# A graph and convolution layer on one core: tap weights transformed channel by channel, and eight neighbour parts moved beside the first frequency products

## The chip, the cores and the metric

The kernel runs on one NeuronCore of a Trainium2 chip, in float32. The metric is device time in microseconds. The run before the change takes 2466.53 us (median of three, 2464.61 to 2470.27). One more execution was recorded by the hardware profiler; the profile and the trace are of that one.

The engines are TensorE (PE; its weight loads are shown apart as PEld), VectorE (DVE), ScalarE (ACT), GpSimd (POOL) and SyncE (SP). Each works through its own queue in the order in which the program issued. SyncE, GpSimd and ScalarE also issue DMAs.

## The reference, cut to what matters

`x` is [128 graphs, 128 nodes, 256 channels], `adj` [128, 128, 128]. The layer that the change touches is the first:

```python
h = relu(layernorm(x))                       # the layer's input, per graph
c = relu(bn1(conv1d(h, conv1_w, pad=0)))     # one tap: a 256x256 product
c = bn2(conv1d(c, conv2_w, pad=8))           # 17 taps along the 128 nodes, 256 -> 256 channels
x_conv = relu(c + h)
s = h @ w_se.T + b_se                        # 3 numbers per node
A = exp(-|s_n - s_m|^2) * adj                # neighbour weights
x_nmp = A @ relu(h @ w_msg.T + b_msg)
x = x + gru([x_conv, x_nmp], h)              # gates r, z, n from w_ih (768x512) and w_hh (768x256)
```

A second layer then works on the first 25 nodes of each graph: five small normalised graph convolutions, summed.

## The kernel before, in words

The 128 graphs are 32 groups q of four (`GB`), in four batches of eight groups (`BQ`). The 17-tap convolution is done in frequency space. A graph's 128 nodes are cut into four overlapping blocks of 48 points (`F`), which a fixed matrix `fwd` transforms; a matrix `inv` transforms back. For each of the 24 frequency pairs the 256x256 product over channels has a real and an imaginary part.

The parts are generators. Each yields a pair: the TensorE time of what it has just issued, and a delay before its next step. `Order.run` (lines 187 to 205) merges two lanes of such generators with these numbers: it picks the lane that is behind by its weight, and in it the generator that is ready first. This sets the order of all instructions when the program is built. Nothing of it is decided on the chip.

- `stage_a(q)`, lines 326 to 372: load x as xa (L318), layernorm on DVE with one small power on POOL, eight transposes ph (L340) and relu to hTa (L342), a store to hTd (L345), the first convolution pc (L351), its bias on DVE (L354) and relu on POOL (L356), then the forward transform pf (L362), copied to X by DVE and ACT (L368, L370).
- `load_taps` and `tap_weights`, lines 375 to 406: four loads of conv2_w, with the 17 taps as partitions, a group of 32 partitions for each quarter of the input channels. Thirty-two steps of four products pw (L394) follow: the constant `tap` [17, 72] is the stationary operand, two input channels with all 256 outputs the moving one. Output partitions are the 72 slots: two for the first pair of frequencies, and three for each of the other 23 (a real part, minus the sum, and a difference). ACT and DVE copy to ws (L401, L399), which has two buffers, and POOL stores it to wfd in DRAM (L403).
- `stage_b(bat)`, lines 409 to 463: for each pair of frequencies load the weights wf from wfd (L418, two DMAs, 1 KB pieces), let POOL form the sum xs of real and imaginary input (L425), and multiply: pa = xs by the first weight (L450), pb = the two parts by the other two (L453). y is the copy pac of pa, added to both halves of pb (L457), and is stored to yd (L459).
- `stage_c(q)`, lines 485 to 635: its first part is the neighbour part: pse (L498), its scaled copies ef (L503, L506), their product lr on POOL (L509), messages pm and msg (L518 to L522), distances pd (L532), transposed adj pt (L534), aT (L536, L537), and x_nmp as px and xnmp (L546, L548). Then it loads yt from yd and transforms back (pi, L562), computes the gates (L581 to L608), transposes back (po, L620), adds x and stores.
- `setup_1`, `prepare`, `block`, from line 640: the second layer, in eight blocks of 16 graphs.

At the start, batch 0's `stage_a` runs beside `tap_weights` (line 875). Then `groups`, which is `stage_c` of all 32 groups, runs beside `side`, which is `stage_b(0)`, then batch 1's `stage_a` and `stage_b`, and so on, at weight 0.5 (line 888); then groups beside the second layer at weight 0.4 (line 889). `stage_c(q)` may begin once group q-1 has its last gates, so beside `stage_b(0)` there is group 0's neighbour part and no other.

Of the kernel before, what the change touches and what calls it, by code (L numbers as in the profile page):

```python
# [9 lines left out]
FP = mybir.dt.float32  # L10
# [9 lines left out]
P = 128  # L20
# [10 lines left out]
NSLOT = 72  # L31
# [29 lines left out]
def _fourier():  # L61
# [8 lines left out]
    tap = np.zeros((TAPS, NSLOT))  # L70
# [17 lines left out]
    for f in range(1, NF + 1):  # L88
        th = 2 * np.pi * ((f * t) % F) / F
        vr, vi = np.cos(th), np.sin(th)  # L90
        tap[:, 3 * f - 1], tap[:, 3 * f], tap[:, 3 * f + 1] = vr, -(vr + vi), vi - vr
    tap4 = np.zeros((P, NSLOT))
# [116 lines left out]
def kernel(ctx: ExitStack, tc: tile.TileContext, x, adj, consts, vecs, w_se, conv1_w,  # L209
# [11 lines left out]

    hTd = [dr.tile([P, 2, 512], FP, name=f"hTd{q}") for q in range(NQ)]
    wfd = dr.tile([NSLOT, D, D], FP, name="wfd")
# [31 lines left out]

    scl, sft = {}, {}
    for bn in ("bn1", "bn2"):
        s = cp.tile([P, 2], FP, name=f"s_{bn}")
        nc.vector.tensor_scalar(s, v(bn + "_v"), EPS, None, op0=ALU.add)
        nc.gpsimd.tensor_tensor(s, s, c("mhalf")[:, :2], ALU.pow)  # L260
        nc.vector.tensor_mul(s, s, v(bn + "_g"))
        t = cp.tile([P, 2], FP, name=f"t_{bn}")
        nc.vector.tensor_mul(t, v(bn + "_m"), s)
        nc.vector.tensor_sub(t, v(bn + "_b"), t)
        scl[bn], sft[bn] = s, t
    brz = cp.tile([P, 4], FP, name="brz")
    nc.vector.tensor_add(brz, v("b_ih")[:, 0:4], v("b_hh")[:, 0:4])


    prow = ptmp.tile([P, 4, P], FP, tag="tmp", name="prow")  # L270
    for i, a in enumerate((scl["bn1"][:, 0:1], scl["bn1"][:, 1:2], sft["bn1"][:, 0:1],
                           sft["bn1"][:, 1:2])):
        wide = f2.tile([P, P], FP, tag="wide", name=f"wide{i}")
        nc.vector.tensor_copy(wide, a.to_broadcast([P, P]))
        nc.tensor.matmul(prow[:, i], wide, ident, start=True, stop=True)
    brow = cp.tile([P, D], FP, name="brow")
    nc.vector.tensor_copy(brow, prow[:, 2:4].rearrange("p a c -> p (a c)"))
    for k in range(2):
        nc.vector.tensor_mul(c1w[:, k], c1w[:, k], prow[:, 0:2].rearrange("p a c -> p (a c)"))


    wse9 = wp.tile([P, 2, WIDE], FP, name="wse9")
    nc.vector.memset(wse9, 0.0)
    for role in range(3):
        nc.vector.tensor_copy(wse9[:, :, 3 * role:3 * role + 3], wse[:, :, :3])
    pbs = ptmp.tile([P, 512], FP, tag="tmp", name="pbs")
    nc.tensor.matmul(pbs[:, :1], c("sel"), v("b_se"), start=True, stop=True)
    bse = cp.tile([P, 1], FP, name="bse")
    nc.vector.tensor_copy(bse, pbs[:, :1])
    emb = c("emb")  # L290
    embb = cp.tile([P, 4], FP, name="embb")
    nc.vector.scalar_tensor_tensor(embb, emb[:, 4:8], bse, emb[:, 8:12],
                                   op0=ALU.mult, op1=ALU.add)
# [14 lines left out]


    lab = ExitStack()  # L310
    ab = lab.enter_context(tc.tile_pool(name="ab", bufs=2, side="right"))
    xf = lab.enter_context(tc.tile_pool(name="xf", bufs=1, side="right"))
    X = xf.tile([P, 2, F, P], FP, name="X")
# [12 lines left out]
    def stage_a(q):  # L326
# [8 lines left out]
        yield 0.0, 8.0  # L335
# [8 lines left out]
        yield 0.9, 2.5  # L344
        nc.gpsimd.dma_start(out=hTd[q], in_=hT)  # L345
        h1 = ab.tile([P, GB, D], FP, tag="h1", name=f"h1{q}")
        for h in range(2):
# [8 lines left out]
            nc.gpsimd.tensor_scalar(h1[:, s], h1[:, s], 0.0, None, op0=ALU.max)  # L356
            yield 1.75, 2.5 * h
# [17 lines left out]
    def load_taps(tw):  # L375

        wts = []
        for n in range(4):
            wt = tw.tile([P, 16, D], FP, tag="wt", name=f"wt{n}", bufs=4)
            src = conv2_w.rearrange("(r n i) t o -> n t r i o", r=4, n=4)[n]  # L380
            for r in range(4):
                nc.sync.dma_start(out=wt[32 * r:32 * r + 16], in_=src[:16, r])
            nc.sync.dma_start(out=wt[16::32], in_=src[16])
            wts.append(wt)
        return wts

    def tap_weights(tw, wts):
        for n in range(4):
            for m in range(8):
                st = tw.tile([NSLOT, 4, 512], FP, tag="ws", name=f"ws{n}_{m}")  # L390
                for r in range(4):
                    pw = pacc.tile([P, 512], FP, tag="acc", name=f"pw{n}_{m}_{r}")
                    rows = slice(32 * r, 32 * r + TAPS)
                    nc.tensor.matmul(  # L394
                        pw[:NSLOT], c("tap")[rows],
                        wts[n][rows, 2 * m:2 * m + 2].rearrange("t i o -> t (i o)"),
                        start=True, stop=True)
                    if r == 3:
                        nc.vector.tensor_copy(st[:, r], pw[:NSLOT])  # L399
                    else:  # L400
                        nc.scalar.activation(st[:, r], pw[:NSLOT], AF.Copy)  # L401
                i0 = 16 * n + 2 * m
                nc.gpsimd.dma_start(  # L403
                    out=wfd.rearrange("s (r i) o -> s r i o", r=4)[:, :, i0:i0 + 2],
                    in_=st.rearrange("s r (i o) -> s r i o", i=2))
                yield 0.9, 1.2


    def stage_b(bat):
        while not all(q in A_DONE for q in range(bat * BQ, (bat + 1) * BQ)):  # L410
            yield 0.0, 0.5
        WF = {}

        def load_w(f):
            w = WF[f] = xf.tile([P, 2, 3, D], FP, tag="wf", name=f"wf{bat}_{f}", bufs=3)
            a, n = (0, 2) if f == 0 else (3 * f - 1, 3)
            for k in range(2):
                nc.sync.dma_start(out=w[:, k, :n],  # L418
                                  in_=wfd[a:a + n, k * P:(k + 1) * P].rearrange("s p o -> p s o"))
# [511 lines left out]
```

## Time and profile before

| what | us |
|---|---|
| median of three runs | 2466.53 |
| the profiled execution, whole | 2468.99 |
| its span, first to last instruction | 2467.2 |
| TensorE busy | 2299.7 (93%) |
| GpSimd, VectorE, ScalarE busy | 790.4, 751.2, 606.6 |
| mean granted clock of TensorE | 0.961 |
| tap products pw, first and last start | 24.7, 177.4 |
| first product of stage b(0) | 212.1 |
| first back transform pi | 300.1 |

A float32 product is two entries for TensorE in this profile, each with its own weight load, so 736 entries of pb are 368 products. A busy TensorE is not always at full speed: PEclk gives the share of the full clock that it was granted. A line such as `PE pd L532 <- POOL lr L509: 17.7, 6, 9.2` says that TensorE waited six times before pd for POOL's lr, 17.7 us in all, the longest 9.2. A line of the chain gives the start, the length, and what ran or was waited for.

### The profile page before, as it was taken

What the parts mean: (1) busy time and instruction counts of PE and PEld (TensorE: products, weight loads), DVE (VectorE), ACT (ScalarE), POOL (GpSimd) and SP (SyncE); (2) the same over time, 40 slices, a digit from 0 to 9 for tenths busy, and PEclk for the clock granted to TensorE, in tenths of its full rate; (3) what the DMA queues carried; (4) which work ended last, traced back from release to release, by engine and by line L of the source; (5) the groups of instructions that cost most, each with busy time, mean ns of one, the idle gap of its engine ahead of it and who ended that gap; (6) DMA issues with size and microseconds to landing.
All of it is one profiled execution on the core that took longest, in us unless ns stands there. A gap on an engine that the chain in (4) does not pass through costs nothing.

```text
span 2467.2 us, 26809 instructions
## 1 busy us (share of the span) xinstructions
PE 2299.7 (93%) x10156; PEld 1509.3 (61%) x10156; DVE 751.2 (30%) x1603; ACT 606.6 (25%) x1149; POOL 790.4 (32%) x976
## 2 busy tenths in 40 slices
PE   3878799998998999999998999999999999999998
PEld 2447655566665666666666666656566665656576
DVE  2333311333223244222343222232232232322343
ACT  1441122222221212222222222222223222232223
POOL 1333323343333234333334333332222232323231
PEclk9779899999999999999999999999999999999999
DMA  9657911233545322555423355611211212120000
GB/s 166 189 164 257 301 43 60 74 89 94 170 159 174 82 52 86 162 179 175 119 77 99 117 171 177 184 44 43 60 38 38 73 31 68 48 55 20 20 21 18
DMA packets 207538, 258.86 MB, mean 105 GB/s; under 512 B 21805, under 2 KB 179378, under 8 KB 207410
## 3 DMA queue, kind: packets, MB, share of 16 engines
q1 hardware_dynamic: 175154, 172.07, 25.8%
q0 software_dynamic: 30208, 81.30, 10.7%
q10 hardware_dynamic: 2048, 3.79, 0.5%
q8 instruction: 80, 1.31, 0.2%
q14 instruction: 48, 0.39, 0.1%
HBM read 175.82 MB, written 81.26 MB: 104 GB/s over the span
## 4 chain that ended last, share of the span: by engine, by line
PE 79%; DMA 3%; DVE 3%; POOL 3%; issue 3%; ACT 2%; SPq 0%; DVEq 0%; POOLq 0%; ACTq 0%
PE pr L581 13%; PE pz L581 13%; PE pn L581 9%; PE pb L453 6%; PE pg L581 4%; PE pi L562 4%; PE pz L812 4%; PE ph L803 4%; PE pc L351 3%; PE pa L450 3%; PE pm L518 3%; PE pf L362 3%; PE px L546 2%; DMA wf<-wfd 1%; PE ph L340 1%
## 5 line engine op out<-in xcount | busy, mean ns | idle before, releaser
L604 POOL TENSOR_TENSOR d<-hT,r 128x512 f32<-128x512 f32 x64 | 80.8, 1263 | 547.6 <-ACT r L596 339.3
L453 PE MATMUL pb<-wf,X 128*128 128x256 f32 x736 | 173.9, 379 | 0.0
L457 DVE TENSOR_TENSOR y<-pac,pb 128x512 f32<-128x512 f32 x92 | 63.2, 687 | 334.1 <-PE pb L453 330.5
L605 POOL TENSOR_TENSOR d<-d,z 128x512 f32<-128x512 f32 x64 | 81.1, 1267 | 257.2 <-ACT z L601 221.1
L453 PEld LDWEIGHTS pb<-wf,X 128*128 128x128 f32 x736 | 139.9, 190 | 19.0
L562 PE MATMUL pi<-cst,yt 96*128 96x64 f32 x1024 | 125.5, 283 | 21.1 <-DMA yt<-yd 21.1
L562 PEld LDWEIGHTS pi<-cst,yt 96*128 96x128 f32 x1024 | 124.2, 201 | 22.8 <-issue 22.6
L596 ACT ACTIVATE r<-r,vec 128x512 f32<-128x512 f32 x64 | 46.2, 722 | 355.5 <-DVE r L595 355.5
L581 PE MATMUL pr<-hT,whh 128*128 128x512 f32 x256 | 129.1, 629 | 0.0
L356 POOL TENSOR_SCALAR h<-h 128x512 f32<-128x512 f32 x64 | 95.5, 1501 | 90.8 <-DVE h L354 90.1
L518 PE MATMUL pm<-wmsg,hT 128*128 128x256 f32 x512 | 122.6, 389 | 2.1 <-ACT ef L506 2.1
L351 PE MATMUL pc<-c1w,hTa 128*128 128x256 f32 x512 | 124.1, 395 | 0.0
L581 PE MATMUL pr<-xnmp,wih 128*128 128x512 f32 x256 | 121.7, 598 | 2.4 <-DVE xnmp L548 2.4
L581 PE MATMUL pr<-xc,wih 128*128 128x512 f32 x256 | 121.1, 595 | 0.0
L581 PE MATMUL pz<-hT,whh 128*128 128x512 f32 x256 | 121.0, 595 | 0.0
L581 PE MATMUL pg<-hT,whh 128*128 128x512 f32 x256 | 120.6, 593 | 0.0
L581 PE MATMUL pn<-xnmp,wih 128*128 128x512 f32 x256 | 120.3, 592 | 0.0
L581 PE MATMUL pz<-xnmp,wih 128*128 128x512 f32 x256 | 120.3, 592 | 0.0
L581 PE MATMUL pz<-xc,wih 128*128 128x512 f32 x256 | 120.3, 592 | 0.0
L581 PE MATMUL pn<-xc,wih 128*128 128x512 f32 x256 | 120.3, 592 | 0.0
L803 PE MATMUL ph<-yz,w 128*128 128x96 f32 (+3 forms) x640 | 113.8, 332 | 4.1 <-ACT aT L536 1.6
L591 DVE SCALAR_TENSOR_TENSOR r<-pg,vec,r 128x512 f32<-128x512 f32 x64 | 48.0, 750 | 228.1 <-PE pg L581 145.8
(156 smaller groups left out, 3771.3 us busy)
## 6 DMA issues: line engine op xcount, KB each, us to landing
wf<-wfd SPq DMA_DIRECT2D x184, 384.0 KB, 4.0
yd<-y POOLq DMA_DIRECT2D x96, 256.0 KB, 4.2
yt<-yd SPq DMA_DIRECT2D x32, 768.0 KB, 7.6
wfd<-ws POOLq DMA_DIRECT2D x32, 576.0 KB, 5.6
xa<-in_x SPq DMA_DIRECT2D x128, 128.0 KB, 4.5
hTd<-hTa POOLq DMA_DIRECT2D x32, 512.0 KB, 3.2
hT<-hTd SPq DMA_DIRECT2D x32, 512.0 KB, 3.4
xt<-in_x SPq DMA_DIRECT2D x128, 128.0 KB, 2.7
```

The lines of the kernel that those rows point to most:

```text
L351: nc.tensor.matmul(pc[:, i], hT[:, k, (2 * h + i) * N:(2 * h + i + 1) * N], c1w[:, k], start=(k == 0), stop=(k == 1))
L356: nc.gpsimd.tensor_scalar(h1[:, s], h1[:, s], 0.0, None, op0=ALU.max)
L362: nc.tensor.matmul(pf[:, i, :F * NB], h1[:, 2 * h + i, k * P:(k + 1) * P], fwd, start=True, stop=True)
L450: nc.tensor.matmul(pa, xs[:, k], w[:, k, 0], start=(k == 0), stop=(k == 1))
L453: nc.tensor.matmul(pb[:, s], X[:, k, 2 * f + part], w[:, k, 1 + s], start=(k == 0), stop=(k == 1))
L518: nc.tensor.matmul(pm[:, i], hT[:, k, j * N:(j + 1) * N], wmsg[:, k], start=(k == 0), stop=(k == 1))
L562: nc.tensor.matmul(pc[:, a * 64:(a + 1) * 64], yt[:, a, co * P:(co + 1) * P], inv[:HB], start=True, stop=True)
L581: nc.tensor.matmul(ps, w, a, start=(i == 0), stop=(i == len(ops) - 1))
L604: nc.gpsimd.tensor_sub(d, hT[:, dc], r)
L605: nc.gpsimd.tensor_mul(d, d, z)
L803: nc.tensor.matmul(ph, w1[:, g, k, m * P:(m + 1) * P], yz[:, k, :, o:o + n], start=(k == 0), stop=(k == 1))
L812: nc.tensor.matmul(pz, w2[:, g, m, cc * P:(cc + 1) * P], hs[g][:, m], start=(m == 0), stop=(m == 3))
```

## The change

Six things change.

1. The tap transform. The input channels become the output partitions. The stationary operand is now the taps of 128 input channels for one output channel (17x128, at a step of 64 floats), the moving one the constant `tap`, now [17, 48]. It is done in two halves k of the input channels, for four quarters r of the output channels, 64 channels each, in seven chunks of 10 or 9 channels. A chunk has four accumulators, and each is copied into ws[r] with its two free axes exchanged. ws[r] has one buffer; a half ends with four stores of [128, 48x64].
2. Two weights are stored for each frequency pair, real and imaginary. Stage b loads both with one DMA (512-byte pieces) and POOL forms the third as their sum. pa now holds the two products of the parts, pb that of the sums, and y is formed by two differences and a sum on DVE.
3. The neighbour part becomes a function of its own, `neighbours`. For groups 0 to 7 a new generator, `early`, runs it beside the end of stage a and beside stage b(0), and stores its result to xmd. `stage_c` loads that in place of adj for these groups. Loads of w_ih and w_hh move from ACT's queue to the end of `tap_weights` on SyncE's.
4. The folding of the batch norms into weights moves from the start of the program into a generator `fold`, the first of the second lane. Stage a's lane has weight 2.
5. The relu after the first convolution goes from POOL to ACT, and lr from POOL to DVE. Some delays in the yields are shorter.
6. In `block`, turn, gather and fuse are issued in a mixed order, the first hidden tile gets a tag of its own (hh0), and zt has three buffers instead of four.

```diff
     for f in range(1, NF + 1):
         th = 2 * np.pi * ((f * t) % F) / F
-        vr, vi = np.cos(th), np.sin(th)
-        tap[:, 3 * f - 1], tap[:, 3 * f], tap[:, 3 * f + 1] = vr, -(vr + vi), vi - vr
+        tap[:, 2 * f], tap[:, 2 * f + 1] = np.cos(th), np.sin(th)
...
+    wfd = dr.tile([P, 8, F, CQ], FP, name="wfd")
+    xmd = [dr.tile([P, 2, 512], FP, name=f"xmd{q}") for q in range(BQ)]
...
-            nc.gpsimd.tensor_scalar(h1[:, s], h1[:, s], 0.0, None, op0=ALU.max)
-            yield 1.75, 2.5 * h
+            nc.scalar.activation(h1[:, s], h1[:, s], AF.Relu)
+            yield 1.75, 1.6 * h
...
+    def tap_weights():
+        mid = ExitStack()
+        tw = mid.enter_context(tc.tile_pool(name="tw", bufs=2))
         wts = []
+        for k in range(2):
+            wt = tw.tile([P, P, CQ], FP, tag="wt", name=f"wt{k}")
+            src = conv2_w[k * P:(k + 1) * P].rearrange("i t (r o) -> r t i o", r=4)
             for r in range(4):
+                nc.sync.dma_start(out=wt[32 * r:32 * r + 16], in_=src[r, :16])
+            nc.sync.dma_start(out=wt[16::32], in_=src[:, 16])
             wts.append(wt)
+        yield 0.0, 4.0
+        bounds = [0, *range(10, CQ + 1, 9)]
+        for k in range(2):
+            ws = [tw.tile([P, F, CQ], FP, tag=f"ws{r}", name=f"ws{k}_{r}", bufs=1)
+                  for r in range(4)]
+            for a, b in zip(bounds, bounds[1:]):
+                pws = [pacc.tile([P, b - a, F], FP, tag="acc", name=f"pw{k}_{a}_{r}")
+                       for r in range(4)]
+                for i in range(a, b):
+                    for r in range(4):
+                        rows = slice(32 * r, 32 * r + TAPS)
+                        nc.tensor.matmul(pws[r][:, i - a], wts[k][rows, :, i], c("tap")[rows],
+                                         start=True, stop=True)
                 for r in range(4):
+                    dst = ws[r][:, :, a:b].rearrange("p s c -> p c s")
+                    if r == 1:
+                        nc.vector.tensor_copy(dst, pws[r])
                     else:
+                        nc.scalar.activation(dst, pws[r], AF.Copy)
+                yield 0.22 * (b - a), 1.5
+            for r in range(4):
+                nc.gpsimd.dma_start(out=wfd[:, 4 * k + r], in_=ws[r])
+        mid.close()
+        wg = ctx.enter_context(tc.tile_pool(name="wg", bufs=1, reuse_waits="tile"))
+        LATE["wih"] = weight(wg, w_ih, [P, 4, 3 * D], "(k p) o -> p k o", "wih", nc.sync)
+        LATE["whh"] = weight(wg, w_hh, [P, 2, 3 * D], "(k p) o -> p k o", "whh", nc.sync)
...
     def stage_b(bat):
...
+        while "xf" not in LATE:
+            yield 0.0, 0.5
+        if bat == 0:
+            yield 0.0, 12.0
...
         def load_w(f):
-            w = WF[f] = xf.tile([P, 2, 3, D], FP, tag="wf", name=f"wf{bat}_{f}", bufs=3)
+            w = WF[f] = xf.tile([P, 8, 3, CQ], FP, tag="wf", name=f"wf{bat}_{f}")
+            nc.sync.dma_start(out=w[:, :, :2], in_=wfd[:, :, 2 * f:2 * f + 2])
...
+        def add(f):
+            XS[f] = xf.tile([P, 2, P], FP, tag="xs", name=f"xs{bat}_{f}", bufs=2)
+            nc.gpsimd.tensor_tensor(XS[f], X[:, :, 2 * f], X[:, :, 2 * f + 1], ALU.add)
+            nc.gpsimd.tensor_tensor(WF[f][:, :, 2], WF[f][:, :, 0], WF[f][:, :, 1], ALU.add)
+
+        def product(ps, xk, f, s):
             for k in range(2):
+                nc.tensor.matmul(ps.rearrange("p (o c) -> p o c", c=CQ), xk(k),
+                                 WF[f][:, 4 * k:4 * k + 4, s], start=(k == 0), stop=(k == 1))
...
+            pa = pacc.tile([P, 2, D], FP, tag="acc", name=f"pa{bat}_{f}")
+            for s in range(2):
+                product(pa[:, s], lambda k: X[:, k, 2 * f + s], f, s)
...
+                nc.scalar.activation(pac, pa, AF.Copy)
+                pb = pacc.tile([P, D], FP, tag="acc", name=f"pb{bat}_{f}")
+                xs = XS.pop(f)
+                product(pb, lambda k: xs[:, k], f, 2)
+                nc.vector.tensor_sub(y[:, 0], pac[:, 0], pac[:, 1])
+                nc.vector.tensor_add(pac[:, 0], pac[:, 0], pac[:, 1])
+                nc.vector.tensor_sub(y[:, 1], pb, pac[:, 0])
...
-        nc.gpsimd.tensor_tensor(lr, ef[:, 0::2], ef[:, 1::2], ALU.mult)
+        nc.vector.tensor_tensor(lr, ef[:, 0::2], ef[:, 1::2], ALU.mult)
...
+    def early(q):
+        while q not in A_DONE:
+            yield 0.0, 0.5
+        if q == 0:
+            load_c(0)
+            yield 0.0, 6.0
+        hT, ad = IN.pop(q)
+        if q + 1 < BQ and q + 1 in A_DONE:
+            load_c(q + 1)
+        xm = LATE["fr"].tile([P, 2, 512], FP, tag="xnmp", name=f"xnmp{q}", bufs=2)
+        yield from neighbours(q, hT, ad, xm)
+        nc.gpsimd.dma_start(out=xmd[q], in_=xm)
...
+        for what, q in ((turn, 0), (turn, 1), (turn, 2), (gather, 0), (gather, 1), (fuse, 0),
+                        (turn, 3), (gather, 2), (fuse, 1), (gather, 3), (fuse, 2), (fuse, 3)):
...
-    with tc.tile_pool(name="tw", bufs=2) as tw:
-        load_xa(0)
-        load_xa(1)
-        taps = load_taps(tw)
-        order.run(Lane([stage_a(q) for q in range(BQ)], ahead=2), Lane([tap_weights(tw, taps)]))
...
-    first, second = [stage_b(0)], [setup_1()]
+    load_xa(0)
+    begin = Lane([stage_a(q) for q in range(BQ)], ahead=2, weight=2.0)
+    beside = Lane([fold(), tap_weights()] + [early(q) for q in range(BQ)])
+    order.run(begin, beside, until=begin)
+    order.run(Lane([stage_b(0)]), beside)
+    first, second = [], [setup_1()]
```

## The prediction

> **What bounds the kernel now.** I read the page's slices first, then busy time by windows, then the chain of waits, then who waits for whom. The slices:
>
> ```profile
> PE   3878799998998999999998999999999999999998
> PEclk9779899999999999999999999999999999999999
> DMA  9657911233545322555423355611211212120000
> ```
>
> A slice is 61.7 us. From the sixth on TensorE is full, so only taking work off it or filling its small gaps helps there. The first five are not full, and their clock is low. The windows:
>
> ```profile
> 20.00:40.00 20.00, 7.74 (x24) 2.33 (x24) 4.92 (x15) 3.12 (x6) 2.61 (x3) 1.00 1.17 108
> 80.00:100.00 20.00, 16.22 (x55) 6.07 (x53) 11.01 (x33) 8.14 (x17) 5.50 (x7) 0.71 0.41 122
> 140.00:160.00 20.00, 16.66 (x54) 6.03 (x52) 10.82 (x33) 7.81 (x16) 5.50 (x7) 0.66 0.42 123
> 240.00:260.00 20.00, 19.24 (x88) 15.97 (x87) 4.81 (x7) 2.93 (x8) 8.52 (x14) 1.00 1.00 338
> 280.00:300.00 20.00, 8.37 (x36) 6.21 (x34) 9.15 (x28) 1.15 (x3) 4.22 (x6) 0.83 0.90 251
> ```
>
> The last three figures are granted clock, DMA share and GB/s. At 20 to 40 us the tap loads fill the DMA at only 108 GB/s; from 60 to 200 us TensorE seems busy, at 0.66 to 0.9 of its clock; at 240 the weight loads of stage b fill the DMA. Who waits:
>
> ```profile
> ACT ws L401 <- DMA wfd<-ws: 74.9, 17, 14.3
> DVE ws L399 <- DMA wfd<-ws: 58.5, 14, 11.9
> PE pw L394 <- ACT ws L401: 34.9, 15, 12.7
> PE pd L532 <- POOL lr L509: 17.7, 6, 9.2
> ```
>
> And the chain:
>
> ```profile
> 158.11 6.11 DMA wfd<-ws
> ...
> 164.33 0.60 ACT ws L401
> ...
> 173.95 5.16 DMA wfd<-ws
> ...
> 232.08 7.29 DMA wf<-wfd
> ...
> 289.73 3.90 DMA yd<-y
> ...
> 293.78 6.16 DMA yt<-yd
> ...
> 300.07 7.06 PE pi L562 x32
> ```
>
> Each of 32 tap steps waits for the staging write of two steps before (133 us of waits on ACT and DVE); stage a's products stand behind it on TensorE. Stage b(0) starts at 212 us, waits for wf four times, and group 0's first inverse product runs at 300.1. By then TensorE did, at full clock: stage a 8 x 7.2 = 57 us (eight transposes 1.0 as in po; eight products 3.65 as in pm; eight of 192 columns 2.6, half of pf's 5.21), taps about 32 x 1.06 = 34, b(0) 62 (a step is 0.86 + 1.73 us in the chain), one neighbour part 7.0 (0.57 + 3.65 + 0.43 + 0.59 + 1.78). That is 160 of 300 us: 140 to win. After it, 2167.1 us hold 2082 us of busy TensorE.
>
> [...] The new tap load has pieces of 256 B (64 floats) instead of 1 KB; no run shows such a load. [...] pd, four row groups, issues its eight loads within 0.31 us, four products in 0.43. [...] The new tap weights are read at a step of 256 B, and evicted at such a step; no row of before does either.
>
> **The change, part by part.** I followed the yields through Lane and Order to get the new order of issue. Times below are on TensorE's clock of events up to group 0's first pi.
>
> *Start.* SyncE now issues xa0, xa1, xa2 before the taps; eight such issues took 8.06 us, so the taps start at about 13 us. One half of the channels is 2.23 MB: 21 us at 107 GB/s. [...] I take 1.3: first tap product at 40 us, between 34 and 56. The tap products stand first in TensorE's queue, ahead of a(1)'s transposes, so nothing hides this. xa3 stands behind both halves on SyncE: it lands near 40 + 27 + 3, and its layernorm (5 us) ends at 75, against a need near 72: 3 us.
>
> *Tap products.* 128 channels-of-four: 512 products of 48 columns with 128 weights, four row groups. pi, of 64 columns, is bound by its loads: 32 of them in 3.65 us later on, two a product, 0.23 us. Below: that pair, perfectly fourfold: 0.23 us a four, 29 us. Above: no overlap, 0.91, 117 us. [...] I take 0.33: 42 us, 8 more than now.
>
> *Evictions.* 56 of 128x432 or 480 instead of 128 of 72x512: about 0.57 on ACT (hh 128x400 is 0.593), 33 us in all instead of 72. All four accumulators belong to one chunk, so two chunks issued one after the other cost about 2.1 us; my order has three such pairs besides the one below, and stage a covers the rest. [...] 14 us, between 6 and 40 (a doubled eviction at the wide step).
>
> *Between the halves.* ws has one buffer for each row group, 1.57 MB each. The first chunk of the second half follows the four writes directly, and its evictions wait for them; behind them on ACT stand hTa's copies of a(4), on TensorE the next chunk and a(4). 32 KB of x1d land in 2.0 us and 512 KB of hTd in 3.2, which is up to 400 GB/s; I take 340, so 6.3 MB and a fixed 2 us are 20.5 us, less the chunk's 3: 18 us idle, between 12 and 28. New, and uncovered.
>
> So stage a and taps end at 40 + 57 + 42 + 14 + 3 + 18 = 174 us, against 212.
>
> *Handover.* The writes of the second half (6.3 MB) run beside wih, whh and the first hT and adj (3.1 MB): 25 us at 370 GB/s, the rate of before at 214 to 290. wf's first load waits for all writes, then 5 us; load_c of group 2 stands behind it on SyncE and is not needed yet. hT comes after some 17 us, so neighbour 0 and half of 1 (9.6 us) fill the gap. First product of b(0) 32 us after the last tap: 206, plus or minus 8.
>
> *b(0) beside neighbours.* 62 + 46 (the other 6.6 parts) = 108 us. Loads fall from 768 to 512 KB a step, but in pieces of 512 B; with yd, hT, adj and xmd 28 MB in 108 us is 260 GB/s, under the 334 of now. POOL's sum of weights (as d, 1.26 us) waits for wf; behind it on POOL stand only the yd issue and the xmd store. I add 8 us for waits (2 to 22): 322. Then yd, yt and group 0: 12 us as now, of which a(9)'s first 2.7 us fill some: pi at 334.
>
> *The rest.* 2167.1 us less seven neighbour parts (49), less a(9)'s 2.7, less half the wait for lr and what relu on POOL (1.5 us against 0.63 on ACT) cost: 10. POOL loses 95.5 + 23.8 us and gains 92 x 1.26 = 116; DVE gains 92 x (3 x 0.41 - 0.69) + 13 = 63 (0.41 from the 128x256 adds); ACT 40 + 20. All lie beside full TensorE (DVE 30%, ACT 25%, POOL 32% busy); if the new sums make TensorE wait, 0 to 15 us, so the gain here is between -5 and 20. Turn, gather and fuse in another order: TensorE's waits there are under 3 us, so nothing. 2105.
>
> Sum: 334 + 2105 = 2439 of span, 1.8 around it (2468.99 - 2467.2): 2441 against 2468.99. The profiled run is 2.5 above the median, so I forecast 2439 against 2466.5, 1.1% faster.
>
> **Rivals.** *Tap loads in small pieces (slower).* Place: wt on SyncE, with xa3 behind. At 2.5 times the time per byte the first half lands at 66, the second at 119, xa3's layernorm is done at 128 against a need at 98: 26 + 27 more than forecast, 2492. It decides from about 1.9 times on; 4 times gives 2556. For: [...] the queue is full at 1.17 already. [...]
> *Tap weights load one after another, or at half rate for the wide step.* At 0.91 us a four, 74 us more, of which waits between the halves and for xa3 absorb 9: 2504. Half rate, fourfold, 0.46 a four, gives 2456. Against: pd's fourfold overlap.
> *The gain is lost to DMA.* Writes at 200 GB/s (12 + 13 us more) and b(0) bound by 512 B pieces (14): 2478 less what neighbours fill, about 2466: no change.
> *More of the old loss goes* ([...] taps 0.23, lr's and relu's waits gone): 2405.
>
> **How the numbers follow.** Forecast 0.55, its own range 2415 to 2460; better 0.06; lost to DMA 0.11; small pieces 0.16; slow weights 0.12. A measurement tells apart some 0.2%, 5 us. Faster: 0.55 less its upper edge, plus 0.06, plus 0.03 from the DMA case: 0.60. Same 0.08, slower 0.32. Range 2400 to 2510: it leaves out part of the better case and the far ends of the slow ones.
>
> **What would show it.** First pw near 40 us (over 50: small pieces); a four of tap products at 0.33; one wait of TensorE of about 18 us in the middle of stage a for ws; first product of b(0) near 206; first pi near 334; no pse, pm or px among groups 0 to 7 later; no wait of pd for POOL. The forecast is wrong if tap loads or tap products hold TensorE, or if after 334 us more than 2125 remain.

## The result, and the profile after

The changed kernel takes 2484.74 us (median of four runs, 2479.94 to 2486.72), the kernel before, in the runs beside it, 2465.57: a ratio of 1.0071, 95% interval 1.0051 to 1.0091. It is 0.7% slower where 1.1% faster was forecast. The profiled execution has a span of 2483.9 us and a mean granted clock of 0.954. One of the five executions of a later version, e15, took 10390 us; its ratio is that of the other four.

The 40 slices of the changed kernel:

```profile
PE   3968989999999889998999999899999999999998
PEclk9768989999999899999999999999999999999999
DMA  9255872335553334444125445212121121212000
```

The second and fifth slices are fuller than before, the third less full, and the clock in the second to fourth is 0.7, 0.6 and 0.8: TensorE is busy there for much of the time, and slow. The same stretches by windows (TensorE, its weight loads, DVE, ACT, POOL; then clock, DMA share, GB/s):

```profile
20.00:40.00 20.00, 2.55 (x10) 2.28 (x10) 6.65 (x31) 0.00 (x0) 1.70 (x2) 1.00 1.26 95
80.00:100.00 20.00, 16.62 (x167) 15.23 (x168) 6.19 (x15) 8.87 (x13) 2.13 (x3) 0.59 0.32 106
140.00:160.00 20.00, 16.97 (x168) 15.48 (x168) 2.88 (x3) 8.51 (x12) 1.06 (x2) 0.59 0.56 194
240.00:260.00 20.00, 20.00 (x122) 17.32 (x121) 12.77 (x21) 5.72 (x13) 13.25 (x16) 1.00 0.83 251
280.00:300.00 20.00, 19.86 (x140) 16.86 (x139) 14.11 (x24) 5.42 (x13) 9.53 (x13) 1.00 0.84 274
```

In the first of them the tap loads, now in 256-byte pieces, run at 95 GB/s where 1 KB pieces ran at 108. In the windows from 80 and from 140 us the mean granted clock is 0.59, with the weight loads (second figure) almost as busy as the products. Stage b(0), from 240, is full (20.00 and 19.86 of 20 us) at a clock of 1.00 in its two windows, as forecast. The waits of TensorE:

```profile
PE pw L404 <- ACT ws L411: 18.1, 6, 8.9
PE px L561 <- DVE aT L553: 18.1, 7, 12.1
PE pw L404 <- DMA wt<-in_conv_w: 17.5, 1, 17.5
...
PE pw L404 <- DVE ws L409: 9.3, 3, 3.5
...
PE pd L548 <- DVE msg L537: 4.0, 2, 2.0
...
PE pd L548 <- DVE lr L525: 3.4, 2, 1.7
```

The waits of pw for ws, on ACT and DVE together, fell from 37.0 us (34.9 and 2.1) to 27.4, of which 18.0 are a new wait between the two halves; pd's wait for lr fell from 17.7 to 3.4. So the waits that the change was to remove did go. The wait of px for aT rose from 7.7 us to 18.1, 12.1 of them in one place, at 1184 us; the same wait of 12.1 us stands in e1, e3, e4, e10, e11 and e16, and no run tries what makes it. From the chain that ended last:

```profile
25.79 15.78 DMA wt<-in_conv_w
...
127.37 14.89 DMA wfd<-ws
...
213.19 5.49 DMA wfd<-ws
...
230.10 4.37 DMA wf<-wfd
...
343.11 6.87 DMA yd<-y
...
351.78 6.37 DMA yd<-y
358.30 5.91 DMA yt<-yd
364.34 5.96 PE pi L610 x32
```

The tap load is in it once, the write of the first half's ws once (at 127), and the end of b(0) is a row of yd, yd, yt. Group 0's first pi comes at 364.3, not at 300.1 as before and not at 334 as forecast; after it 2119.6 us remain, where before it was 2167.1 and 2105 were forecast. Stage by stage against the forecast's own sum:

| step | forecast, us | measured, us | difference |
|---|---|---|---|
| first tap product | 40 | 41.7 | +1.7 |
| from there to the end of stage a and taps | 134 | 170.0 (to 211.7) | +36.0 |
| handover to b(0)'s first product | 32 | 22.8 (to 234.5) | -9.2 |
| b(0) | 116 | 113.2 (to 347.7) | -2.8 |
| to group 0's first pi | 12 | 16.6 (to 364.3) | +4.6 |
| the rest | 2105 | 2119.6 | +14.6 |
| sum (span) | 2439 | 2483.9 | +44.9 |

Two rows make the miss: the tap stage and the rest. Together they are 50.6 us over; that the handover and b(0) were priced 12 us too high hides a part of it.

### The profile page after: what moved, and what is told of

The parts are those of the page before. It is cut to its first block, busy times and chain, and to the rows that moved or that the text cites. A ratio compares the mean times of both kernels' runs of the same rounds, so it can differ in the third digit from the quotient of the medians.

```text
span 2483.9 us, 28406 instructions
## 1 busy us (share of the span) xinstructions
PE 2310.1 (93%) x10924; PEld 1563.8 (63%) x10924; DVE 886.1 (36%) x1801; ACT 634.8 (26%) x1145; POOL 778.2 (31%) x956
## 4 chain that ended last, share of the span: by engine, by line
PE 78%; DVE 6%; issue 5%; DMA 4%; POOL 3%; ACT 3%; SPq 1%; DVEq 0%; POOLq 0%; ACTq 0%
PE pr L630 13%; PE pz L630 12%; PE pn L630 9%; PE pa L449 6%; PE pc L357 5%; PE pi L610 4%; PE pg L630 4%; PE ph L853 4%; PE pz L862 4%; PE pf L368 3%; PE pb L449 3%; PE px L561 2%; PE pm L534 2%; PE pw L404 1%; PE ph L346 1%
## 5 line engine op out<-in xcount | busy, mean ns | idle before, releaser
L653 POOL TENSOR_TENSOR d<-hT,r 128x512 f32<-128x512 f32 x64 | 81.1, 1267 | 507.1 <-ACT r L645 280.2
L449 PE MATMUL pa<-wf,X 128*128 128x256 f32 x768 | 188.2, 389 | 9.4 <-DMA wf<-wfd 9.4
L449 PEld LDWEIGHTS pa<-wf,X 128*128 128x128 f32 x768 | 147.9, 196 | 53.8 <-issue 28.4
L473 DVE TENSOR_TENSOR y<-pac 128x256 f32<-128x256 f32 x92 | 65.0, 707 | 275.8 <-ACT pac L469 273.5
L654 POOL TENSOR_TENSOR d<-d,z 128x512 f32<-128x512 f32 x64 | 81.1, 1268 | 230.0 <-ACT z L650 196.2
L444 POOL TENSOR_TENSOR wf<-wf 128x512 f32<-128x512 f32 x92 | 123.8, 1346 | 46.2 <-DMA wf<-wfd 46.1
L357 PE MATMUL pc<-c1w,hTa 128*128 128x256 f32 x512 | 135.3, 424 | 0.0
L272 POOL TENSOR_TENSOR rs<-rs,cst 128x4 f32<-128x4 f32 x40 | 40.8, 1021 | 294.1 <-DVE rs L271 294.1
L357 PEld LDWEIGHTS pc<-c1w,hTa 128*128 128x128 f32 x512 | 108.9, 216 | 24.9 <-issue 5.8
L650 ACT ACTIVATE z<-pz,brz 128x512 f32<-128x512 f32 x64 | 44.0, 687 | 282.0 <-PE pz L630 282.0
```

Source lines behind the costliest of these rows:

```text
L357: nc.tensor.matmul(pc[:, i], hT[:, k, (2 * h + i) * N:(2 * h + i + 1) * N], c1w[:, k], start=(k == 0), stop=(k == 1))
L444: nc.gpsimd.tensor_tensor(WF[f][:, :, 2], WF[f][:, :, 0], WF[f][:, :, 1], ALU.add)
L449: nc.tensor.matmul(ps.rearrange("p (o c) -> p o c", c=CQ), xk(k), WF[f][:, 4 * k:4 * k + 4, s], start=(k == 0), stop=(k == 1))
L473: nc.vector.tensor_sub(y[:, 0], pac[:, 0], pac[:, 1])
L653: nc.gpsimd.tensor_sub(d, hT[:, dc], r)
L654: nc.gpsimd.tensor_mul(d, d, z)
```

## The experiments

Differences in us are those of the ratios to the kernel before, times 2466; the changed kernel itself stands at +17.5 by that measure. The intervals reach 0.0011 to 0.0021 to each side, 3 to 5 us. Times of a stage come from one profiled execution of each version, and these vary too: in the changed kernel, e4, e6, e9 and e10, whose tap stage is the same, the last tap product starts between 206.8 and 211.4 us.

### The wide step of the tap weights

In e1 the stationary operand is read in a row instead of at a step of 256 bytes. The products then use other numbers (the taps of other channels), so the convolution is another one; the work is the same.

```diff
-  nc.tensor.matmul(pws[r][:, i - a], wts[k][rows, :, i], c("tap")[rows], ...)
+  nc.tensor.matmul(pws[r][:, i - a], wts[k][rows].rearrange("t i c -> t (i c)")[:, i * P:(i + 1) * P],
+                   c("tap")[rows], ...)
```

> The changed kernel, but the tap products read their 128 stationary columns side by side instead of at a step of 64 floats (same count, same bytes, other channels, so the frequency weights are others). The changed kernel takes 2484.7 us and a chunk of nine fours takes 4.15 us, 0.46 a four. Theory A, the wide step makes the weight load slow: a load falls from 305 to about 190 ns, a four to about 0.30, 128 fours save 20 us, 2465. Rival, the four is bound by eight loads and eight products being issued, or by the low clock: 0.46 stays, 2485.

2463.94 us, ratio 0.9995 (0.998 to 1.0009): 19 us less than the changed kernel, by this one operand. TensorE's timeline in the changed kernel (start, length, group; in brackets the idle time before it and its releaser):

```profile
65.80 4.15 PE L404 MATMUL pw<-cst,wt 17*128 17x48 f32 x72
69.88 5.49 PE L368 MATMUL pf<-cst,h 128*128 128x192 f32 x16
...
85.37 4.15 PE L404 MATMUL pw<-cst,wt 17*128 17x48 f32 x66 [2.83 <-DVE ws L409]
89.45 3.42 PE L346 MATMUL ph<-cst,xa 128*128 128x128 f32 x16
92.81 4.17 PE L404 MATMUL pw<-cst,wt 17*128 17x48 f32 x72
96.91 10.03 PE L357 MATMUL pc<-c1w,hTa 128*128 128x256 f32 x32
...
112.07 4.13 PE L404 MATMUL pw<-cst,wt 17*128 17x48 f32 x72
```

and the same stretch of e1:

```profile
65.48 2.22 PE L404 MATMUL pw<-cst,wt 17*128 17x48 f32 x72
67.63 2.87 PE L368 MATMUL pf<-cst,h 128*128 128x192 f32 x16
...
88.64 2.22 PE L404 MATMUL pw<-cst,wt 17*128 17x48 f32 x72
90.80 7.17 PE L357 MATMUL pc<-c1w,hTa 128*128 128x256 f32 x32
97.81 5.37 PE L368 MATMUL pf<-cst,h 128*128 128x192 f32 x32
...
107.95 3.60 PE L404 MATMUL pw<-cst,wt 17*128 17x48 f32 x74 [0.31 <-ACT ws L411]
...
132.51 4.07 PE L404 MATMUL pw<-cst,wt 17*128 17x48 f32 x66 [3.04 <-ACT ws L411]
```

The weight loads of these products, in the changed kernel and then in e1 (shortest, median and longest, ns; first and last start):

```profile
L404 PEld LDWEIGHTS pw<-cst,wt x1024: 286/305/308, 41.7 to 211.3; 17*128 17x128 f32 x171
L404 PEld LDWEIGHTS pw<-cst,wt x1024: 181/187/333, 41.8 to 192.9; 17*128 17x128 f32 x171
```

A chunk of nine channels is 36 products, 72 entries. At the wide step it takes 4.15 us, 0.46 us a four. In a row it takes 2.22, 0.247 a four, close to the 0.23 that the forecast read from pi for perfect overlap. This holds at full clock: from 112.1 to 116.1 us the changed kernel's granted clock is 1.00, and the chunk takes 4.13. From 143.4 to 147.4 the clock is 0.50, and a chunk there takes 4.13 as well. In a row it takes 4.07 in the last line of e1, where the clock is 0.50 (the window from 120 to 140 us has 0.51 on the mean). So the low clock alone doesn't explain the slow chunks, and where the clock is down the wide step costs next to nothing. In e1 seven of the fourteen chunks take 2.22 us. Of the other seven, which take longer, five have the low clock for all or part of their time (in the windows of 20 us that start at 60, 80, 100, 120 and 160 us e1 has 0.87, 0.79, 0.72, 0.51 and 0.50 on the mean); two stand at the start, on which see the last section.

The second effect is on what follows. The chunk at 65.80 us has no idle time ahead of it, and TensorE is busy throughout; the granted clock is 1.00 up to 68.5 us and 0.50 from 69.0 on. The pf behind it takes 5.49 us, where in e1, behind the quick chunk, it takes 2.87. Likewise pc at 96.91 takes 10.03 us at a mean clock of 0.70, and in e1 7.17 at 1.00. Only the step differs between the two kernels, so the slow chunks also cost clock for their neighbours; by what rule is not shown. e1 isn't rid of the low clock: from 100 to 120 us, where TensorE is busy for 9.84 us, it is 0.72 on the mean, and from 120 to 140, with 9.46 us busy, 0.51. About the same chunk takes 3.60 us in the line at 107.95, and one pc in e1, behind a chunk at a clock of 0.50, takes 9.09.

With the weights in a row the last tap product starts at 192.9 us instead of 211.4, and pi comes at 346.7.

### The evictions at the same step

e2 stores ws without the exchange of axes (another order in memory, so other weights for stage b).

```diff
-  dst = ws[r][:, :, a:b].rearrange("p s c -> p c s")
+  dst = ws[r].rearrange("p s c -> p (s c)")[:, a * F:b * F].rearrange("p (c s) -> p c s", s=F)
```

> The changed kernel, but the tap evictions write ws side by side, without exchanging the axes (the frequency weights are stored in another order). Theory A, the step of 256 B is what makes an ACT copy take 992 ns: it falls to about 600, DVE's 1094 to about 500, the two stalls of 6 us between chunks in a row shrink to about 2, and the whole falls by 8 to 12 us, to about 2474. Rival, stage a's products cover the evictions: under 3 us.

2483.17 us, ratio 1.0071 (1.0054 to 1.0088): nothing. The copies did get shorter, on ACT from a median of 992 ns to 531, on DVE from 1094 to 608, but the whole doesn't. The stall for DVE ahead of the chunk at 85 us, 2.83 us, is 4.21 in e2: in the changed kernel DVE's eviction (r = 1) stands behind two layernorms, which hold DVE from 74.60 to 84.44 us, and its own length isn't what is waited for.

### The wait between the two halves

e3 puts a delay behind the four stores of the first half, so that stage a's next products are issued ahead of the chunk that waits.

```diff
                 nc.gpsimd.dma_start(out=wfd[:, 4 * k + r], in_=ws[r])
+            if k == 0:
+                yield 0.0, 20.0
```

> The changed kernel with a delay of 20 planned us after the four stores of the first half, so that groups 4 and 5 of stage a are issued before the second half's first chunk. Theory B, the single buffer of ws costs what the gap shows: the 22 us gap of TensorE at 121 to 143 us closes to under 4, the first product of b(0) comes some 18 us earlier than 234.5, the whole is 2466. Rival, the gap is only moved: the evictions or the second half's stores are late by as much, b(0) starts at 230 or later, 2480 or more.

2472.79 us, ratio 1.003 (1.0018 to 1.0041): 10 us less, of the 18 that were expected; b(0) starts at 221.2 us instead of 234.5. In the changed kernel the wait is four pieces:

```profile
132.31 0.67 PE L404 MATMUL pw<-cst,wt 17*128 17x48 f32 x2 [8.91 <-ACT ws L411]
135.98 0.66 PE L404 MATMUL pw<-cst,wt 17*128 17x48 f32 x2 [3.00 <-DVE ws L409]
139.70 0.66 PE L404 MATMUL pw<-cst,wt 17*128 17x48 f32 x2 [3.06 <-ACT ws L411]
143.39 4.13 PE L404 MATMUL pw<-cst,wt 17*128 17x48 f32 x66 [3.03 <-ACT ws L411]
```

8.91 + 3.00 + 3.06 + 3.03 = 18.0 us. The copies that free the accumulators wait for the stores of the first half (ACT 21.6 us, DVE 7.9), and so one accumulator comes free for each store that lands. That is the 18 us of the forecast. An order of issue alone takes 10 us off the whole.

### y on VectorE

e4 reads the first operand of y's two first sums from PSUM instead of from the copy.

```diff
-  nc.vector.tensor_sub(y[:, 0], pac[:, 0], pac[:, 1])
-  nc.vector.tensor_add(pac[:, 0], pac[:, 0], pac[:, 1])
+  nc.vector.tensor_sub(y[:, 0], pa[:, 0], pac[:, 1])
+  nc.vector.tensor_add(pac[:, 0], pa[:, 0], pac[:, 1])
```

> The changed kernel, but y's first difference and the sum take their first operand from the accumulator pa instead of its copy, so that no operation of y has two operands in SBUF; the result is the same. Theory C, VectorE's operations with two SBUF operands wait for GpSimd's sums and hold it up: the mean of y's first difference falls from 707 to about 420 ns, VectorE's busy time by some 80 us, the end of b(0) up to group 0's pi (347 to 364 us) shortens by about 5, the whole falls by 8 to 15 us, to about 2473. Rival, all of it lies beside full TensorE: busy time falls, the whole stays within 3 us of 2484.7.

2468.46 us, ratio 1.0017 (1.0004 to 1.003): 13 us less. The groups of VectorE (busy us, mean ns; then the idle time ahead of them) in the changed kernel:

```profile
L474 DVE TENSOR_TENSOR pac<-pac 128x256 f32<-128x256 f32 x92 | 72.6, 789 | 3.2
L473 DVE TENSOR_TENSOR y<-pac 128x256 f32<-128x256 f32 x92 | 65.0, 707 | 275.8 <-ACT pac L469 273.5 <-DMA yd<-y 2.3
...
L525 DVE TENSOR_TENSOR lr<-ef 128x256 f32<-128x256 f32 x32 | 25.9, 808 | 20.1 <-ACT ef L522 16.3 <-DMA wfd<-ws 3.7
```

and in e4:

```profile
L473 DVE TENSOR_TENSOR y<-pa,pac 128x256 f32<-128x256 f32 x92 | 39.1, 425 | 306.6 <-ACT pac L469 302.5 <-DMA yd<-y 4.1
L474 DVE TENSOR_TENSOR pac<-pa,pac 128x256 f32<-128x256 f32 x92 | 38.2, 415 | 0.0
L525 DVE TENSOR_TENSOR lr<-ef 128x256 f32<-128x256 f32 x32 | 29.5, 921 | 20.0 <-ACT ef L522 16.3 <-DMA wfd<-ws 3.7
```

With the first operand in PSUM the mean falls from 707 and 789 ns to 425 and 415. The timeline of the changed kernel shows what stands beside the long ones. Where an operation of GpSimd on tiles (L443, L444, L653, L654 or L656) overlaps them, they take 0.81 us on the mean (67 of y) and 1.06 (53 of pac); where none does, 0.42 (25 and 39), and never more than 0.43. For instance, an addition of pac that starts at 343.81 us takes 2.16 us; it ends 0.30 us after the second of two sums on GpSimd, which run from 343.71 to 345.67. So two inputs in SBUF alone cost no more here; lr, of the same size, takes 425 ns in the median on VectorE in e13 below, where no weight sum runs on GpSimd. The third line shows that lr, also with two inputs in SBUF, gets longer in e4, from 808 to 921 ns. After pi, 2104.3 us remain in e4, against 2119.6 in the changed kernel, and 2121.7 and 2117.4 in e1 and e3, where this stretch is unchanged. pi comes at 356.0, 8 us earlier, but 5 of these lie ahead of b(0) (its first product is at 229.6 instead of 234.5), where e4 changes nothing.

### Part 5: relu to ScalarE, lr to VectorE

The forecast counted a gain of 10 us here. e7 makes the two moves alone, in the kernel before:

```diff
-  nc.gpsimd.tensor_scalar(h1[:, s], h1[:, s], 0.0, None, op0=ALU.max)
+  nc.scalar.activation(h1[:, s], h1[:, s], AF.Relu)
-  nc.gpsimd.tensor_tensor(lr, ef[:, 0::2], ef[:, 1::2], ALU.mult)
+  nc.vector.tensor_tensor(lr, ef[:, 0::2], ef[:, 1::2], ALU.mult)
```

> The kernel before with two operations moved alone: relu of h1 from POOL to ACT, lr from POOL to DVE. The forecast's term: TensorE's wait for lr (17.7 us) halves and relu's shorter time helps stage a: 10 us, 2456. Rival, the waits are taken up by what is late next (msg, ef, or the layernorm): within 3 us of 2465.

2482.15 us, ratio 1.0065 (1.005 to 1.008): 16 us slower. So the two were taken apart, undone one at a time in the changed kernel (e9, e10) and done one at a time in the kernel before (e13, e14).

> The changed kernel with the relu of h1 back on GpSimd; lr stays on VectorE. Theory A (the relu on ScalarE is what cost 17 us in the kernel before with both moved: it stands in ScalarE's queue behind other work and holds it up where stage a runs beside full TensorE): 10 to 16 us faster than the changed kernel, about 2472. Theory B (it was lr on VectorE): within 4 us of the changed kernel, 2481 to 2489. Theory C (GpSimd, now with the weight sums too, 1.26 us each, becomes late): slower by 5 or more, over 2490.

> The changed kernel with lr back on GpSimd; the relu stays on ScalarE. Theory A (relu is the loss): within 4 us of the changed kernel, or slower by up to 10 since lr waits behind GpSimd's weight sums. Theory B (lr on VectorE stands behind VectorE's queue, and TensorE waits for it before pd): 6 to 14 us faster, about 2474.

> The kernel before with lr alone on VectorE (relu stays on GpSimd). Both together cost 17 us there. Theory A (lr is the loss, as in the changed kernel, where putting lr back gave 9 us and the relu 3): 10 to 17 us slower than before, about 2478. Theory B (the two add: each costs its share): 5 to 9 us slower. Theory C (relu is the loss in the kernel before): within 4 us of before.

> The kernel before with the relu of h1 alone on ScalarE (lr stays on GpSimd). Theory A (lr is the loss): within 4 us of before. Theory B (they add): 5 to 9 us slower. Theory C (relu is the loss): 10 to 17 us slower.

| | us | ratio (interval) | against its base |
|---|---|---|---|
| e9: changed kernel, relu back | 2481.63 | 1.0068 (1.005 to 1.0086) | -1 |
| e10: changed kernel, lr back | 2475.16 | 1.0035 (1.002 to 1.005) | -9 |
| e13: before, lr alone moved | 2481.98 | 1.0065 (1.0048 to 1.0083) | +16 |
| e14: before, relu alone moved | 2463.98 | 0.9996 (0.9985 to 1.0007) | -1 |

It is lr, and within the intervals lr alone. On VectorE the product itself is quicker (425 ns against 728 on GpSimd, medians of the kernel before and e13). What it does to its queue is seen in a group's neighbour part after stage b's products; VectorE in the changed kernel:

```profile
1035.28 0.41 DVE L519 TENSOR_SCALAR ef<-pse,cst,embb 128x128 f32<-128x128 f32 x1 [0.59 <-ACT ef L522]
1036.21 1.84 DVE L525 TENSOR_TENSOR lr<-ef 128x256 f32<-128x256 f32 x1 [0.53 <-ACT ef L522]
1037.97 0.68 DVE L537 TENSOR_TENSOR msg<-pm,bmsg 128x512 f32<-128x512 f32 x1
...
1041.16 0.68 DVE L537 TENSOR_TENSOR msg<-pm,bmsg 128x512 f32<-128x512 f32 x1
```

GpSimd there:

```profile
1036.20 1.27 POOL L444 TENSOR_TENSOR wf<-wf 128x512 f32<-128x512 f32 x1
```

and VectorE in e10:

```profile
1031.09 0.41 DVE L519 TENSOR_SCALAR ef<-pse,cst,embb 128x128 f32<-128x128 f32 x1 [0.59 <-ACT ef L522]
1031.42 0.68 DVE L537 TENSOR_TENSOR msg<-pm,bmsg 128x512 f32<-128x512 f32 x1
...
1035.64 0.68 DVE L537 TENSOR_TENSOR msg<-pm,bmsg 128x512 f32<-128x512 f32 x1
```

In the changed kernel VectorE stands 0.53 us for ScalarE's last ef, then 1.84 us in lr, beside GpSimd's sum of the weights (1036.20 to 1037.47); the first msg, whose products ended at 1034.3, starts 2.69 us after ef instead of 0.33. TensorE waits for the second msg before pd: 1.98 us there, 0.64 in e10. This queue is a part of the loss. Over the stretch after pi, TensorE is idle for 85.3 us in the changed kernel and 80.2 in e10, and busy 2034.3 and 2029.9.

In the kernel before no weight sum runs on GpSimd, and lr's longest in e13 is 532 ns; the wait for ef remains, 32 times, 16.8 us in all. But the trace of e13 doesn't show the 16 us as waits of TensorE: after pi it is idle for 85.0 us in the kernel before and 87.2 in e13. What grows is the busy time, from 2082.1 to 2092.5. What makes it grow is not shown, and the cause of e13's loss stays open.

### What the early neighbour parts are worth, and the old staging

e6 takes part 3 out of the changed kernel: b(0) runs in the side lane, as before, and all groups have their neighbour part in `stage_c`. e8 gives the kernel before a third staging buffer for ws.

> The changed kernel without the early neighbour parts: groups 0 to 7 compute theirs in stage c as before, b(0) runs beside group 0 as before. Theory D, they fill gaps of TensorE (some 10 us at the handover) and shield b(0) from its load waits: without them the whole is 2495 to 2500. Rival, they are only moved, and crowd VectorE and POOL beside b(0): 2480 to 2487.

> The kernel before with three staging buffers ws instead of two. By the forecast's reading staging is what holds the first 212 us: a step then waits for the write of three steps before, stage b(0) starts near 180 instead of 212, the whole is 2435. Rival, with staging eased the layernorms, ACT's copies and the low clock hold it: under 10 us, 2457 or more.

e6: 2535.4 us, ratio 1.0278 (1.0259 to 1.0297), 51 us slower than the changed kernel. Its pi comes at 316.3, 48 us earlier, but 2218.6 us remain after it, 99 more. Seven parts of 7 us of TensorE's time are 49; moved back beside full groups they cost twice that. pd's waits for msg and lr are 37.8 us in e6 against 7.4 in the changed kernel; the rest of the 99 was not traced. So 51 us is what the early parts are worth in this kernel, with y and lr on a crowded VectorE; in a repaired one it was not tried. e8: 2459.47 us, ratio 0.9977 (0.9966 to 0.9988), 6 us instead of the 30 that the forecast's reading gave. The waits of ACT and DVE for the staging writes fall from 133 us to 77, and stage b(0) starts at 204.3 instead of 212.1. So a third buffer is worth little; what more buffers would give the kernel before was not tried.

### Versions that beat both

e5 is the changed kernel with the tap transform of the kernel before (output channels as moving columns, loads in 1 KB pieces), but with 48 slots and six staging buffers. e12 adds y from PSUM, e16 also lr back on GpSimd. e11 keeps the new transform, with three repairs: conv2_w laid out with output channels ahead of input channels, which makes the weights contiguous and the load's pieces 512 bytes; e3's delay; e4's sums. e15 adds lr back.

> The changed kernel with the tap transform of the kernel before (frequencies as output partitions, the constant stationary, 512 columns moving, loads in 1 KB pieces), with 48 slots and six staging buffers; stage b loads the two weights of a pair with two DMAs. All else as changed. Theory A, the new transform is what costs: 32 steps of 1.06 us are 34 us of TensorE instead of 58, the clock stays up, nothing waits between halves, and stage a with the taps ends near 150 us instead of 212; the whole is 2425. Rival, ACT's 96 copies of 0.59 us and stage a's own bind, or staging waits again: stage a ends at 180 or later, the whole is 2455 or more.

> The changed kernel with three repairs: the tap weights in a row (conv2_w laid out on the host with output channels ahead of input channels, so that both the stationary operand and the load pieces are contiguous, 512 B), the 20 us delay before the second half's first chunk, and the first product sum of y read from PSUM. Alone the three measured -21, -12 and -16 us against the changed kernel. Theory A (they lie in three different places, so they add): -45 to -50, about 2438. Theory B (the delay and the faster tap products fill the same gap, so that they overlap): -35, about 2450.

> The changed kernel with the old transform of 48 slots (as in the earlier run, 2432.3) and y's first sums read from PSUM as well. Theory A (the two losses are in different places, they add): another 14 to 18 us less, about 2417. Theory B (without the late first half of the kernel VectorE has slack): within 5 us of 2432.

> The changed kernel with the three repairs (2434.5) and lr back on GpSimd. Theory A (lr on VectorE costs 9 us whatever stands around it): about 2425. Theory B (with y read from PSUM VectorE has slack, so that lr is early enough there): within 4 us of 2434.

> The changed kernel with the old transform of 48 slots and y read from PSUM (2429.1), and lr back on GpSimd. Theory A: about 2420. Theory B: within 4 us of 2429. Both are well below the kernel before.

| | us | ratio (interval) |
|---|---|---|
| e5: old transform, 48 slots | 2432.3 | 0.9862 (0.9845 to 0.9878) |
| e12: e5 and y from PSUM | 2429.1 | 0.9846 (0.9828 to 0.9864) |
| e16: e12 and lr on GpSimd | 2415.18 | 0.9785 (0.9765 to 0.9806) |
| e11: new transform, three repairs | 2434.49 | 0.9875 (0.9859 to 0.9891) |
| e15: e11 and lr on GpSimd | 2426.2 | 0.9837 (0.9816 to 0.9857) |

The three repairs give 48 us together, 19 + 10 + 13 = 42 one by one: they add, within the intervals. In e11 the last tap product starts at 176.0, pi at 326.9, and 2105.3 us remain. In e12 y from PSUM gave only 4 us where 14 to 18 were expected if the losses added. lr's mean rose there from 897 to 1060 ns, but it rose in e4 too (808 to 921), so this alone doesn't say why the two differ. Taking lr off VectorE then gave 15 (in e15, against e11, 9). Of these versions e16 is the fastest, 2.15% under the kernel before. So of the change's parts the early neighbour parts pay (e6). The two weights a frequency are in every version that beats the kernel before, but were not taken out by themselves. The new tap transform doesn't pay: even repaired it is 7 us behind the old one with 48 slots (e11 against e12, whose intervals just overlap), and 13 us with lr back on GpSimd (e15 against e16).

## Why the prediction was wrong

**First tap product, 40: right** (41.7). The rival of small tap-load pieces falls: 95 GB/s against 108, no factor of two. The factor of 1.3 on this load was the author's estimate; no run of before has a load in such pieces.

**Stage a and the taps, 57 + 42 us: the step that failed.** A four of tap products was put at 0.33 us, between one of pi (0.23) and of pd (0.43), and stage a at 57 us "at full clock". Both terms were too small. The wide step, half rate at 0.46 a four, was named as a rival for 2456, and its rate was exact: 0.46 a four, 59 us for 128 fours. But its price left out the clock. The forecast's own windows, from 80 and from 140 us, showed 0.71 and 0.66 beside the taps, and in the changed kernel it is 0.59 there. From the first tap product to the last, in us of TensorE:

| | forecast | changed kernel | e1 | e11 |
|---|---|---|---|---|
| tap products | 42 | 66.3 | 49.7 | 44.6 |
| stage a | 57 | 77.9 | 68.6 | 72.1 |
| waits (14 + 3 + 18) | 35 | 27.7 | 34.9 | 21.6 |

The first two rows overlap by some 2 us. In the changed kernel tap products and stage a are 24 and 21 us over, and the waits 7 under. Weights in a row take 17 us off the first row and 9 off the second (4 against e4, whose tap stage is that of the changed kernel), and 7 come back as waits. Even so a four costs 0.39 us on the average of e1, since half of its chunks take longer: with contiguous weights too 0.33 would have been too little.

**Evictions covered, 14 us for those in a row: the mechanism was right.** The 14 us were the author's estimate. The copies are nearly twice as long at the wide step (992 ns against 531 on ACT; a doubling was the upper bound of that step), but e2 shows that their length isn't what is waited for.

**Between the halves, 18 us: right** (18.0, in four pieces).

**Handover 32, b(0) 116: 9 and 3 us too high.** The handover, 22.8, lies just outside its plus or minus 8. (The rate of before at 214 to 290 us, given there as 370 GB/s, is 341 by windows.) The rival in which the gain is lost to DMA falls: in the two windows of b(0) TensorE is busy for 20.00 and 19.86 us at a clock of 1.00, with the DMA at 251 and 274 GB/s.

**To the first pi, 12 us: 16.6.** The chain has two yd stores in a row there, of 6.87 and 6.37 us, where the kernel before has one of 3.90: the last y waits 2.26 us for an earlier store to land. Shorter sums of y don't change that: in e4 the same stretch takes 15.9 us.

**The rest, 2105: 14.6 us too low.** Two terms of it failed. The forecast priced y's additions at 0.41 us each and said that VectorE's 63 us lie beside full TensorE; two of the three took 0.71 and 0.79 beside GpSimd's sums, which the same paragraph adds to GpSimd. It did allow 0 to 15 us for the case that the new sums make TensorE wait, but counted none. And "half the wait for lr and what relu on POOL cost: 10" was counted as a gain. The wait of pd for lr did go (17.7 to 3.4), yet lr on VectorE costs 9 us in this kernel and 16 in the one before, and relu's move is worth nothing measurable. Nothing in that step asked what is queued behind the instruction that was moved; in the group shown msg is, but the whole of the loss is not traced to it. e4's 2104.3 shows the size of the first term; e10's 2110.0 (2474.0 less 364.0) that of the second.

**The check on the whole.** With three repairs e11 stands at 326.9 + 2105.3 = 2432.2, against the forecast's 334 + 2105. Its tap stage takes 135.6 us from first to last product, against 134. This agreement is in part luck: in the table stage a is 15 us over and the waits 13 under, for e11's delay fills a wait that the forecast counted in full; and lr's loss is still in the 2105.3. What the forecast had right are the start, the wait between the halves, and b(0). The sign was lost on the price of two access patterns, on the clock beside the first of them, and on the move of lr.

## What to carry to other kernels

When a change turns a constant operand into one read at a wide step, try the price of double, which this operand had at full clock (4.13 us against 2.22 for 36 products), and ask what the slower stage does to the clock of its neighbours: here the operand cost 19 us, and part of it was paid by products that were not touched. Don't price a stage at full clock where the windows of the kernel before show 0.66 to 0.71. A move to a quicker engine is not yet a gain: lr got 303 ns quicker in the median and cost 9 and 16 us. Look at what the moved instruction waits for, and what stands behind it in its new queue. When GpSimd gets long sums over SBUF, go through VectorE's instructions with two SBUF inputs, and see which of them can take one input from PSUM; in e4 this gave 13 us, while lr, which kept both, got longer (808 to 921 ns).

## What the runs showed of the hardware that was not expected

A float32 stationary operand of 17x128 read at a step of 256 bytes has a median weight load of 305 ns in this trace, against 187 in a row, and at full clock nearly doubles the time of a stream of four-row-group products: 4.13 us against 2.22 for 36 of them. At a granted clock of 0.50 the two take 4.13 and 4.07: the time at the wide step was the same at both clocks. On the write side, copies at a step of 256 bytes took longer as well: by the medians of e2 and the changed kernel 531 against 992 ns on ACT, and 608 against 1094 on DVE.

The granted clock can be low, and can fall, while the records show TensorE full. In e11's window from 80 to 100 us it is busy for all 20.00 us, at 0.70; in the changed kernel it falls from 1.00 to 0.50 between 68.5 and 69.0 us, inside a chunk at the wide step with no idle time. So a full slice in the first line of the page is no proof of full speed; the second line has to be read with it.

Nor is the second line proof at the start of a run. Between 49.8 and 53.9 us e1's chunk in a row takes 4.09 us, about what one takes at a granted clock of 0.50 (4.07), while the view gives a clock of 1.00 from 40 to 60 us. In the changed kernel a pc takes 9.35 us from 53.92 us on, at 1.00 by the view, where e1's at 90.80 takes 7.17. What holds them up is not shown. So the 1.00 in the first windows of this document and of the forecast should not be leaned on.
